# TensorE drains as release points: what message products, pairs and gathers wait for in a graph-network kernel

## The chip, the core and the metric

The kernel runs on one core of a Trainium2 chip. The core has five engines with a queue of their own each: TensorE (PE) for matrix products, VectorE (DVE), ScalarE (ACT), GpSimd (POOL) and SyncE (SP). They tell each other of finished work by semaphores. Sixteen DMA engines move data. The metric is the device time of one execution in microseconds (us), lower is better.

## The reference: what is computed

One message-passing block on a graph of 1,250 nodes with 512 features each (3 x 128 vector parts and 128 scalars) and 40,000 edges sorted by their target node, then a residual with layer norm:

```python
def _painn_block(x, edge_index, edge_attr1, edge_attr2, W1, b1, W2, b2, W3, b3, U, V, ...):
    x_j = x[src]
    v_j = x_j[:, :384].reshape(E, 128, 3)
    s_j = silu(x_j[:, 384:] @ W1 + b1) @ W3 + b3
    rbf = jnp.sqrt(2.0 / R_CUT) * jnp.sin(n * jnp.pi * r / R_CUT) / r
    cutoff = 0.5 * (jnp.cos(jnp.pi * r / R_CUT) + 1.0) * (r < R_CUT)
    edge_basis = rbf * cutoff @ W2 + b2            # 20 -> 384 for each edge
    s1, s2, s3 = split of (s_j * edge_basis)
    v_msg = v_j * s1[:, :, None] + s3[:, :, None] * edge_attr1[:, None, :]
    x = x + segment_sum([v_msg, s2], dst)          # first pass over the edges
    x_j = x[src]                                   # second pass: per node, then per edge
    v, v_V, norm, h = ...                          # U, V, a small network on (norm, s)
    msg = [v * s1, dot(v, v_V) + s3]               # depends on the source node alone
    return x + segment_sum(msg, dst)
x = layernorm(x + block(x, ...))
```

The second pass sends a row that depends on the source node alone. So the kernel doesn't gather for it: during the first pass it counts the links between nodes into a matrix, and multiplies the nodes' rows by these counts later.

## The kernel before, in words

**Tiling.** The 40,000 edges are cut into 80 batches (NT), of four tiles of 128 edges as a rule. Four batches make a group, and two groups a block of 128 target nodes. For each tile POOL issues one indirect DMA (`gather`, L756) that fetches 128 source rows of 640 numbers (2,560 bytes) from a table in device memory into one of five rooms in SBUF, which are parts of the tiles `more` (three) and `nodes` (two). POOL gathers three batches ahead.

**One step of the main loop** (step t, within `windowed`; its loop is at L1701) does this:

- DVE, `messages(t)`: the product of the gathered scalars with the edge factors (L916) and that of the vector parts (L918). Both read the factors from PSUM, where there is one set of four banks, `eb`. Then DVE compares numbers to make `pair` (L939, for the links; there are two buffers), `hot` (L847) and `spread` (L859, both for the additions).
- PE, `add_messages(t-1)`: 4 + 12 products (L955, L961) that sum the messages by target into `agg`. Their left sides are one-hot matrices of 32 columns.
- PE, `count_links(t-1)`: four products (L984) that count links into `adj`; L976 carries the part that two groups share. In the steps that the set `behind` holds, this stands after the factors and gathers, in all others before them.
- PE, `edge_factors(t+1)`: four products, one for each tile (L906; each runs in two parts in the profile's count, so "x8"), that write the next batch's factors to `eb`. They can't start before L918 of step t has read the banks.
- POOL, `gather(t+3)`: four gathers. The first of them waits for the last product of `edge_factors(t+1)`, and for the addition that last read the room.

Around these stand lists of further work (`first`, `early`, `late`, `mid`, `dve`, `amid`) that close a group (ACT copies the sums, L997 to L1024), turn the next edges' basis (L823, L828) and run the node network (L1051 to L1360). ACT also makes the one-hot matrices `one` from L871 and L881 for the links.

**What sets the order.** Each engine runs its own instructions in the order in which the program writes them. A tile library adds the semaphore waits from what is read and written; a wait that an engine has already passed at a later count isn't added again. A product that somebody waits for raises a semaphore of PE's (PE_49) when it completes. For the last three batches there are two smaller sets of banks (`halves`).

## Time and profile before

| | |
|---|---|
| Median of 3 runs | 569.23 us (568.55 to 569.3) |
| The profiled execution's own time | 567.24 us |
| Its span in the profile | 565.4 us |
| Granted clock of TensorE, mean | 0.907 |
| PE busy | 444.6 us (79%) |
| DVE busy | 432.1 us (76%) |
| ACT busy | 377.0 us (67%) |
| POOL busy | 350.1 us (62%) |
| Gather queue's packets, share of the 16 DMA engines | 62.6% |

The profile is of one execution. "Span" is the time from its first to its last instruction; what lies around it, 567.24 less 565.4 us, is 1.84 us. An engine's busy time leaves out waits. Ends of matrix products are modelled, not seen, so what a product's waiters did tells more of its end than its own row. A row of the timeline gives the start, the duration, the engine, the line, what is written and read, and in brackets how long the engine had been idle and what ended that. "issue" there means that the profile shows nothing that was waited for, "remote" that no releaser on this core was found. Granted clock 1.00 is PE's full speed; in parts of the span less is granted.

### The profile page before, as it was taken

To read this page: it belongs to the slowest core of one execution; us is meant where nothing else is said; L and a number is where in the kernel's file an instruction comes from. 1 tells how busy PE (TensorE), PEld (TensorE's weight loads), DVE (VectorE), ACT (ScalarE), POOL (GpSimd) and SP (SyncE) were. 2 spreads that over 40 slices of the span, in tenths; PEclk is the share of its full clock that TensorE was granted. 3 is DMA by queue.
4 is the path that set the end of the run, shared out by engine and by line. 5 is a ranking of instruction groups with operands and counts; after the bars stand their busy time and mean duration, and the time that the engine had idled before them with its cause. 6 is when DMAs were issued, how large, how long until landed. Compare 5 with 4: busy or idle time off the path is not lost.

```text
span 565.4 us, 11226 instructions
## 1 busy us (share of the span) xinstructions
PE 444.6 (79%) x4257; PEld 249.3 (44%) x4257; DVE 432.1 (76%) x660; ACT 377.0 (67%) x955; POOL 350.1 (62%) x377
## 2 busy tenths in 40 slices
PE   8557667677878787767887797879789698989993
PEld 6323233353344344435433443545445354445682
DVE  5576687778877877886778778787878887797675
ACT  3493565567777566775757687577768766788663
POOL 7775666666666666665556665666666666574530
PEclk9856998979897979988788897999989999999997
DMA  8786777777777776776777787678778777877413
GB/s 247 269 243 188 227 228 221 226 214 227 234 222 203 239 223 214 228 230 192 209 217 217 205 258 231 193 234 250 220 237 229 236 224 223 265 217 237 157 56 133
DMA packets 37938, 123.29 MB, mean 218 GB/s; under 512 B 7296, under 2 KB 9870, under 8 KB 37874
## 3 DMA queue, kind: packets, MB, share of 16 engines
q0 software_dynamic: 25824, 104.47, 62.6%
q1 hardware_dynamic: 10850, 17.35, 9.3%
q8 instruction: 35, 0.57, 0.4%
q10 hardware_dynamic: 1200, 0.66, 0.4%
q14 instruction: 29, 0.24, 0.2%
HBM read 112.94 MB, written 9.51 MB: 217 GB/s over the span
## 4 chain that ended last, share of the span: by engine, by line
PE 55%; DVE 20%; ACT 13%; issue 6%; another core or an unknown queue 3%; DMA 2%; POOL 0%; SPq 0%; DVEq 0%; POOLq 0%
PE eb L906 11%; PE agg L955 8%; PE agg L961 6%; DVE more L918 5%; PE adj L984 5%; PE begun L1359 5%; ACT one L881 5%; DVE nodes L918 4%; DVE more L916 3%; PE work L1146 3%; DVE nodes L916 3%; PE work L1051 2%; PE work L823 2%; ACT one L871 2%
## 5 line engine op out<-in xcount | busy, mean ns | idle before, releaser
L756 POOL DMA_INDIRECT more<-table,src_i x189 | 188.8, 999 | 106.2 <-issue 43.0
L756 POOL DMA_INDIRECT nodes<-table,src_i x124 | 123.5, 996 | 68.4 <-issue 28.6
L881 ACT ACTIVATE one<-one,weight,src_f 128x128 f16<-128x128 f16 x313 | 128.6, 483 | 0.2
L916 DVE TENSOR_TENSOR more<-more,eb 128x1024 f32<-128x1024 f32 (+2 forms) x48 | 57.2, 1193 | 63.8 <-PE eb L906 29.9
L871 ACT ACTIVATE one<-number,low 128x128 f16<-128x128 f16 x313 | 99.8, 393 | 6.9 <-remote 4.6
L906 PE MATMUL eb<-w_sb,basis_t 21*128 21x384 f32 x614 | 78.9, 577 | 29.4 <-DVE more L918 14.5
L918 DVE TENSOR_TENSOR more<-more,eb 128x1536 f32<-128x1536 f32 (+2 forms) x48 | 81.8, 1705 | 0.0
L916 DVE TENSOR_TENSOR nodes<-nodes,eb 128x1024 f32<-128x1024 f32 x30 | 36.6, 1222 | 39.4 <-PE eb L906 21.3
L955 PE MATMUL agg<-more,hot 128*32 128x512 f32 x378 | 61.7, 687 | 5.2 <-ACT sums L1006 5.2
L961 PEld LDWEIGHTS agg<-more,spread 128*32 128x32 f32 x1134 | 39.6, 119 | 37.8 <-issue 36.6
L984 PE MATMUL adj<-pair,one 128*128 128x160 f16 x313 | 38.0, 243 | 22.6 <-DVE basis L814 18.7
L918 DVE TENSOR_TENSOR nodes<-nodes,eb 128x1536 f32<-128x1536 f32 x30 | 52.4, 1747 | 0.0
L961 PE MATMUL agg<-more,spread 128*32 128x128 f32 x1134 | 48.6, 291 | 2.7 <-issue 2.7
L906 PEld LDWEIGHTS eb<-w_sb,basis_t 21*128 21x128 f32 x614 | 26.5, 198 | 51.9 <-issue 22.8
L859 DVE TENSOR_TENSOR spread<-hot,carried 128x384 f32<-128x384 f32 (+1 forms) x81 | 44.4, 549 | 2.7
L955 PE MATMUL agg<-nodes,hot 128*32 128x512 f32 x248 | 40.6, 658 | 3.9 <-ACT sums L1006 3.8
L984 PEld LDWEIGHTS <-one 128*128 128x128 f16 x313 | 23.4, 103 | 38.3 <-issue 36.4
L939 DVE TENSOR_TENSOR pair<-number,column 128x640 f16<-128x640 f16 (+1 forms) x81 | 38.7, 479 | 0.0
L961 PEld LDWEIGHTS agg<-nodes,spread 128*32 128x32 f32 x744 | 25.5, 118 | 23.1 <-issue 22.7
L961 PE MATMUL agg<-nodes,spread 128*32 128x128 f32 x744 | 31.8, 289 | 1.0 <-issue 0.9
L828 ACT COPY basis_t<-work 128x512 f32<-128x512 f32 x20 | 11.7, 587 | 29.6 <-PE adj L984 12.3
L1359 PE MATMUL begun<-upper,cast 128*128 128x512 f32 x57 | 28.1, 493 | 0.2 <-ACT cast L1350 0.2
(289 smaller groups left out, 711.2 us busy)
## 6 DMA issues: line engine op xcount, KB each, us to landing
table<-more SPq DMA_DIRECT2D x10, 320.0 KB
more<-table,src_i POOLq DMA_INDIRECT x189
spilled<-begun SPq DMA_DIRECT2D x10, 256.0 KB
more<-spilled SPq DMA_DIRECT2D x2, 1280.0 KB
node_x<-in_x_dram SPq DMA_DIRECT2D x35, 64.0 KB
nodes<-table,src_i POOLq DMA_INDIRECT x124
out_dram<-more SPq DMA_DIRECT2D x7, 256.0 KB
nodes<-in_x_dram POOLq DMA_DIRECT2D x2, 768.0 KB
```

Of the source, the lines that this page charges most:

```text
L756: got = nc.gpsimd.indirect_dma_start(out=rows_t[:n, j, :], out_offset=None, in_=sh.table1, in_offset=bass.IndirectOffsetOnAxis(ap=sh.src_i ...
L859: nc.vector.tensor_mul(spread[t][:m, js], hots[t][:m, js, None, :].to_broadcast(shape), sh.attr[:m, g, e : e + n, :, None].to_broadcast(sh ...
L871: nc.scalar.activation(onehots[t][:, j, :], number[:, :P], AF.Abs, bias=low[:, e : e + 1])
L881: nc.scalar.activation(one, one, AF.Relu, scale=less[:, e : e + 1], bias=worth[:, e : e + 1])
L906: made = nc.tensor.matmul(made_in[t][:, j, :V], turned[g][rows, i, :], sh.w2_sb[rows, :], start=True, stop=True,)
L916: nc.vector.tensor_mul(msg[:m, js, V:], msg[:m, js, V:], factors_of(t, js)[:m, :, C:V])
L918: nc.vector.tensor_mul(msg[:m, js, :V].rearrange("p t (k c) -> p t k c", k=3), msg[:m, js, :V].rearrange("p t (k c) -> p t k c", k=3), fac ...
L939: nc.vector.tensor_tensor(pair[:m, js, :].rearrange("p t (l h) -> p t l h", h=2), number[:m, : PARTS * WIN].rearrange("p (l h) -> p l h", ...
L955: nc.tensor.matmul(agg[j * WIN : (j + 1) * WIN, :], hots[t][:, j, :], msg[:, j, :width], start=(i == 0), stop=False, skip_group_check=True,)
L961: nc.tensor.matmul(agg[j * WIN : (j + 1) * WIN, c * C : (c + 1) * C], spread[t][:, j, c, :], msg[:, j, width:], start=False, stop=(i == la ...
L984: nc.tensor.matmul(to[:, :, at : at + WIN], one[:m, j, :], pair[:m, j, :].rearrange("e (p n) -> e p n", n=WIN), start=(i == 0 and j == js[ ...
L1359: nc.tensor.matmul(acc, casts[a, b], rows[:, a, :], start=(start and a == first and k == 0), stop=(stop and a == end - 1 and k == 1),)
```

## The change

PE gets a drain (`nc.tensor.drain()`), an instruction of its own that waits for the engine's work, behind each batch's factors (80 drains), and one behind the links' products in 33 steps: those before a step of the set `behind`, and the last ones. What waited for products waits for drains now:

- The message products (L916 and L918 before) are told not to depend on the factors' products, and wait for the drain.
- `pair` is told not to depend on the link products of two batches before, which read its buffer, and waits for their drain, or for that of its own batch's factors where there is none.
- All four gathers of a batch wait for the drain; before, the first alone waited for the last product. They are told not to depend on the additions that last read the room.

The order of the instructions stays the same on every engine; what they wait for differs. On POOL, the gathers of one batch stand so in the program of before (PE_49 is the semaphore that products raise, DMASW those of earlier gathers):

```order
L756 DMA more<-table_169,src_i 128x640 [waits DMASW2_49,DVE_49,PE_49]
L756 DMA more<-table_169,src_i 128x640 [waits DMASW3_49]
L756 DMA more<-table_169,src_i 128x640 [waits DMASW4_49]
L756 DMA more<-table_169,src_i 128x640 [waits DMASW5_49]
L756 DMA more<-table_169,src_i 128x640 [waits DMASW6_49,DVE_49,PE_49]
```

and so, from the eleventh batch on, in the changed one:

```order
L758 DMA more<-table_169,src_i 128x640 [waits PE_sequencer_49,DMASW2_49,DVE_49,PE_49]
L758 DMA more<-table_169,src_i 128x640 [waits DMASW3_49,PE_49]
L758 DMA more<-table_169,src_i 128x640 [waits DMASW4_49,PE_49]
L758 DMA more<-table_169,src_i 128x640 [waits DMASW5_49,PE_49]
L758 DMA more<-table_169,src_i 128x640 [waits PE_sequencer_49,DMASW6_49,DVE_49,PE_49]
```

PE_sequencer_49 is the semaphore that drains raise. The wait on PE_49 that each gather has now is for the last addition of a room's reader ten batches earlier. On DVE, a step's work begins so in the program of before:

```order
L916 TENSOR_TENSOR more<-more,eb_403 128x4x256 [waits DMASW6_49,DMASW1_49,DMASW7_49,DMASW0_49,PE_49]
L918 TENSOR_TENSOR more<-more,eb_403 128x4x384
L814 TENSOR_TENSOR basis<-turn,adj 128x16x20 [waits PE_49,Activation_49]
L939 TENSOR_TENSOR pair<-number,column 128x640
L847 TENSOR_TENSOR hot<-lane,carried 128x128
L859 TENSOR_TENSOR spread<-hot,carried 128x384 [waits DVE_49]
```

and so in the changed one:

```order
L931 TENSOR_TENSOR more<-more,eb_403 128x4x256 [waits DMASW6_49,DMASW1_49,DMASW7_49,DMASW0_49,PE_sequencer_49]
L935 TENSOR_TENSOR more<-more,eb_403 128x4x384
L819 TENSOR_TENSOR basis<-turn,adj 128x16x20 [waits PE_49,Activation_49]
L956 TENSOR_TENSOR pair<-number,column 128x640 [waits PE_sequencer_49]
L852 TENSOR_TENSOR hot<-lane,carried 128x128
L864 TENSOR_TENSOR spread<-hot,carried 128x384 [waits DVE_49]
```

In other steps `pair` waits for a link product itself (PE_49), in 40 of them where 21 did before. Of the additions (L987 in the changed kernel) 280 raise the semaphore, where 26 did. The factors' drain is L917 there, the links' L1017.

```diff
--- before.py
+++ after.py
@@ -742,6 +742,7 @@
 
         rows_of, msgs, onehots, turned, hots, spread = {}, {}, {}, {}, {}, {}
         aggs, adjs, pairs = {}, {}, {}
+        makers, tells, adders, counters = {}, {}, {}, {}
 
         sync = mybir.DependencyInfo(mybir.DependencyClass.Sync, mybir.DependencyReason.DATA)
 
@@ -751,6 +752,7 @@
 
             g, i = batches[t]
             rows_t = next(rooms)
+            past = t - len(sh.rooms)
             for j in tiles(g, i):
                 n = lanes(g, i, j)
                 got = nc.gpsimd.indirect_dma_start(
@@ -761,11 +763,14 @@
                         ap=sh.src_i[:n, g, i * CPG + j : i * CPG + j + 1], axis=0
                     ),
                 )
-                if behind is not None and j == 0:
-                    tc.add_manual_dep(
-                        got.ins, behind.ins.name, sync,
-                        reason="so that rows come while PE is ahead of DVE",
-                    )
+                if behind is None:
+                    continue
+                tc.add_manual_dep(
+                    got.ins, behind.ins.name, sync,
+                    reason="so that rows come while PE is ahead of DVE",
+                )
+                for made in adders.get(past, ()):
+                    tc.declare_no_dep(got.ins, made.ins, reason="a later drain is waited for")
             clear_rest(t, rows_t, nc.gpsimd)
             rows_of[t] = rows_t
 
@@ -901,25 +906,37 @@
 
         def edge_factors(t):
             g, i = batches[t]
+            makers[t] = []
             for j in tiles(g, i):
                 rows = slice(j * FEAT, j * FEAT + N_RBF + 1)
                 made = nc.tensor.matmul(
                     made_in[t][:, j, :V], turned[g][rows, i, :], sh.w2_sb[rows, :],
                     start=True, stop=True,
                 )
-            return made
+                makers[t].append(made)
+            tells[t] = nc.tensor.drain()
+            return tells[t]
+
+        def behind_drain(t, reader):
+            for made in makers[t]:
+                tc.declare_no_dep(reader.ins, made.ins, reason="a drain behind them is waited for")
+            tc.add_manual_dep(
+                reader.ins, tells[t].ins.name, sync, reason="TensorE drains behind a batch's factors"
+            )
 
         def messages(t):
             g, i = batches[t]
             msg = rows_of.pop(t)
             for js, n, m in runs(g, i):
-                nc.vector.tensor_mul(msg[:m, js, V:], msg[:m, js, V:], factors_of(t, js)[:m, :, C:V])
+                behind_drain(t, nc.vector.tensor_mul(
+                    msg[:m, js, V:], msg[:m, js, V:], factors_of(t, js)[:m, :, C:V]
+                ))
             for js, n, m in runs(g, i):
-                nc.vector.tensor_mul(
+                behind_drain(t, nc.vector.tensor_mul(
                     msg[:m, js, :V].rearrange("p t (k c) -> p t k c", k=3),
                     msg[:m, js, :V].rearrange("p t (k c) -> p t k c", k=3),
                     factors_of(t, js)[:m, :, None, :C].to_broadcast([m, n, 3, C]),
-                )
+                ))
             run(amid, t)
             make_pair(t)
             if t == 0:
@@ -936,7 +953,7 @@
             for js, n, m in runs(g, i):
                 e = g * EPG + i * CPG + js.start
                 shape = [m, n, PARTS * WIN // 2, 2]
-                nc.vector.tensor_tensor(
+                compared = nc.vector.tensor_tensor(
                     pair[:m, js, :].rearrange("p t (l h) -> p t l h", h=2),
                     number[:m, : PARTS * WIN].rearrange("p (l h) -> p l h", h=2)[
                         :, None
@@ -944,6 +961,14 @@
                     column[:m, e : e + n, None, :].to_broadcast(shape),
                     op=ALU.is_equal,
                 )
+                if t - 2 in counters:
+                    made, drained = counters[t - 2]
+                    for mm in made:
+                        tc.declare_no_dep(compared.ins, mm.ins, reason="a later drain is waited for")
+                    tc.add_manual_dep(
+                        compared.ins, (drained or tells[t]).ins.name, sync,
+                        reason="TensorE drains behind a batch's links",
+                    )
             pairs[t] = pair
 
         def add_messages(t):
@@ -951,19 +976,20 @@
             if i == 0:
                 aggs[g] = ps_sum.tile([P, width], F32, name="agg")
             agg, msg, js = aggs[g], msgs.pop(t), tiles(g, i)
+            adders[t] = []
             for j in js:
-                nc.tensor.matmul(
+                adders[t].append(nc.tensor.matmul(
                     agg[j * WIN : (j + 1) * WIN, :], hots[t][:, j, :],
                     msg[:, j, :width], start=(i == 0), stop=False, skip_group_check=True,
-                )
+                ))
             for c in range(3):
                 for j in js:
-                    nc.tensor.matmul(
+                    adders[t].append(nc.tensor.matmul(
                         agg[j * WIN : (j + 1) * WIN, c * C : (c + 1) * C],
                         spread[t][:, j, c, :], msg[:, j, width:],
                         start=False, stop=(i == last_tile(g, j) and c == 2),
                         skip_group_check=True,
-                    )
+                    ))
 
         def count_links(t):
 
@@ -977,16 +1003,18 @@
                     to[:, :, : REACH - GSPAN], ident, passed.pop(g),
                     start=True, stop=False, skip_group_check=True,
                 )
+            made = []
             for j in js:
                 m = lanes(g, i, j)
                 at = j * SHARE
 
-                nc.tensor.matmul(
+                made.append(nc.tensor.matmul(
                     to[:, :, at : at + WIN], one[:m, j, :],
                     pair[:m, j, :].rearrange("e (p n) -> e p n", n=WIN),
                     start=(i == 0 and j == js[0] and g == 0), stop=(i == last_tile(g, j)),
                     skip_group_check=True,
-                )
+                ))
+            counters[t] = made, nc.tensor.drain() if t + 1 in behind or t + 2 >= NT - 3 else None
 
 
         def close_group(g):
```

## The prediction

> **What bounds the kernel now.** I read the head of the profile's page first, with its chain of waits (the columns of the engine rows: busy time, share of the span, instructions).
>
> ```profile
> span 565.4 us, 11226 instructions
> PE 444.6 (79%) x4257; PEld 249.3 (44%) x4257; DVE 432.1 (76%) x660; ACT 377.0 (67%) x955; POOL 350.1 (62%) x377
> PEclk9856998979897979988788897999989999999997
> PE 55%; DVE 20%; ACT 13%; issue 6%; another core or an unknown queue 3%; DMA 2%; POOL 0%; SPq 0%; DVEq 0%; POOLq 0%
> ```
>
> No engine is full; the chain goes round between PE and DVE. So a step is waited for, rather than an engine being short. The table of busy times by stretch tells how long a batch takes. Its columns: the stretch and its length, then busy us (and instructions) of PE, PE's weight loads, DVE, ACT and POOL, the granted clock, the DMA engines' share and GB/s.
>
> ```profile
> 35.00:515.00 480.00, 380.83 (x3922) 204.78 (x3921) 374.74 (x528) 328.67 (x848) 308.03 (x312) 0.91 0.76 224
> 187.10:193.12 6.02, 4.38 (x37) 2.04 (x37) 4.58 (x6) 2.55 (x7) 3.84 (x4) 1.00 0.81 237
> 193.12:199.22 6.10, 4.52 (x56) 1.99 (x54) 5.69 (x9) 5.87 (x16) 4.16 (x4) 1.00 0.76 235
> 205.37:212.28 6.91, 6.42 (x52) 3.59 (x52) 4.71 (x6) 4.71 (x13) 3.82 (x4) 0.55 0.74 209
> 224.44:230.52 6.08, 5.28 (x59) 3.21 (x60) 4.84 (x7) 5.89 (x14) 3.83 (x4) 1.00 0.74 220
> ```
>
> The first row is the main loop: 312 gathers in 480 us, four to a batch, so 78 batches of 6.15 us, with PE busy 380.83/78 = 4.88 us in each. The other rows are single batches. At the full clock a batch takes 6.0 to 6.1 us whether PE has 4.4 or 5.3 us of work in it; only at the lower clock (0.55) does PE fill it, 6.42 of 6.91. A clock of 0.91 on average, with 0.55 where it is low, means 0.09/0.45 = a fifth of the loop, some 14 batches of 6.9 us; the other 64, at 6.0 us, make up the 480.
>
> What holds those 64 at 6.0 us is in the timeline (start, duration, engine, line, operation; in brackets the idle time before it and what ended that).
>
> ```profile
> 187.36 1.22 DVE L916 TENSOR_TENSOR nodes<-nodes,eb 128x1024 f32<-128x1024 f32 x1 [1.18 <-remote]
> 187.59 0.96 POOL L756 DMA_INDIRECT more<-table,src_i  x1 [1.11 <-remote]
> 188.50 1.75 DVE L918 TENSOR_TENSOR nodes<-nodes,eb 128x1536 f32<-128x1536 f32 x1
> 188.86 0.96 POOL L756 DMA_INDIRECT more<-table,src_i  x1 [0.30 <-issue]
> 190.12 0.96 POOL L756 DMA_INDIRECT more<-table,src_i  x1 [0.30 <-issue]
> 190.30 0.93 PE L906 MATMUL eb<-w_sb,basis_t 21*128 21x384 f32 x8 [1.33 <-issue]
> 191.15 1.12 PE L1051 MATMUL work<-sums,sel 128*128 128x512 f32 x2
> 191.39 0.96 POOL L756 DMA_INDIRECT more<-table,src_i  x1 [0.30 <-issue]
> 192.47 1.12 PE L1051 MATMUL work<-sums,sel 128*128 128x512 f32 x2 [0.19 <-issue]
> 193.38 1.22 DVE L916 TENSOR_TENSOR more<-more,eb 128x1024 f32<-128x1024 f32 x1 [1.40 <-PE work L1051]
> 193.61 0.96 POOL L756 DMA_INDIRECT more<-table,src_i  x1 [1.27 <-PE work L1051]
> ...
> 196.58 0.48 DVE L939 TENSOR_TENSOR pair<-number,column 128x640 f16<-128x640 f16 x1
> 196.83 0.93 PE L906 MATMUL eb<-w_sb,basis_t 21*128 21x384 f32 x8
> 199.48 1.22 DVE L916 TENSOR_TENSOR more<-more,eb 128x1024 f32<-128x1024 f32 x1 [0.38 <-PE adj L984]
> ...
> 202.42 0.93 PE L906 MATMUL eb<-w_sb,basis_t 21*128 21x384 f32 x8 [0.67 <-DVE more L918]
> 205.63 1.22 DVE L916 TENSOR_TENSOR more<-more,eb 128x1024 f32<-128x1024 f32 x1 [0.99 <-remote]
> ...
> 211.55 0.93 PE L906 MATMUL eb<-w_sb,basis_t 21*128 21x384 f32 x8
> 212.40 1.06 PE L955 MATMUL agg<-more,hot 128*32 128x512 f32 x8
> 212.54 1.22 DVE L916 TENSOR_TENSOR nodes<-nodes,eb 128x1024 f32<-128x1024 f32 x1 [2.17 <-PE eb L906]
> ```
>
> The factors of a batch (L906) end by the page at 191.23, 197.76 and 203.35; the message product that reads them (L916) starts at 193.38, 199.48 and 205.63: 2.15, 1.72 and 2.28 us later, though DVE was idle for 1.40, 0.38 and 0.99 us of it, and POOL's first gather starts 0.23 us behind DVE. The wait is credited to products that came after L906, or to "remote", since L906 had long been done. In the slow-clock batch the gap is 0.06 us (212.48 to 212.54). So **the signal of a product, not the product, is late** in the full-clock batches. That results lie ready sooner is likely, though not shown. The view of line L916 by releaser says how much of DVE's waiting this is:
>
> ```profile
> L916 DVEq EVENT_SEMAPHORE  x157: 21/50/3945, 32.3 to 522.9; - x157
>   PE eb L906: 51.2, 30
>   remote: 16.4, 14
>   PE adj L984: 10.9, 13
>   PE begun L1359: 9.0, 7
>   PE work L1051: 7.0, 5
> ```
>
> The last four rows, 43.3 us in 39 batches, are idle time that ended with something other than the factors.
>
> **The change part by part.** The sum is made against the profiled execution, 567.24 us (span 565.4); the median of the runs, 569.23, is 2.0 above it, which I add at the end. No instruction changes place; waits and drains are all that is new. L917, L956, L758, L987 and L1017 are lines of the changed kernel, all others those of the one before.
>
> *Factors' drain (L917, 80 of them) and the message products behind it.* Gain per batch at the full clock: 6.0 less what limits it next. The ring through the one set of factor banks is L916 and L918, 187.36 to 190.25, then L906 to 191.23: 3.87 us, and the drain's own time, not the limit. POOL is: four gathers of 0.96 + 0.30 make 5.04, and 0.23 to restart behind a signal gives 5.3. DVE has 4.58 to 5.69 us of work, ACT up to 5.89. So a plain batch can lose at most 0.7 us, and one like the two rows with ACT at 5.9 only 0.1 to 0.2; ACT's mean, 328.67/78 = 4.2 us, says that these are few, and I take a quarter. Upper bound: 48 x 0.7 + 16 x 0.2 = 37 us; lower: 0, if the drain tells nobody sooner. I take 0.5 and 0.15, as PE's 5.28 and a drain make some 5.5 in the fuller batches: 24 + 2 = **26 us less**. The 43.3 us of late releases above have room for that.
>
> *The same drains on PE.* No row shows a drain between products. Bounds: nothing where PE waits anyway (1.33 us ahead of L906 at 190.30), and 2.15 us if it lasts as long as the signal does. Nearest is the gap of 0.19 us at 192.47, where products do not follow without a seam; with the first weight load no longer under the product before it (0.08 us of overlap between L906's end at 212.48 and L955's start at 212.40) about 0.3 us. At the full clock this lies in PE's idle 0.8 to 1.6 us of a batch. In the 14 slow-clock batches PE is nearly full: 14 x 0.3 = **4 us more**. Queued behind a drain stand the additions of a batch (L955) or, as here, a closing group's products (L1051), and ACT's copies of the sums wait for those.
>
> *Links' drain (L1017, 33).* Of the same price, in the steps where links stand behind factors, so a second seam for PE: 33 x 0.3 = 10 us if nothing covers it, hidden where PE has 0.8 us to spare, and a fifth of the steps are slow-clock ones: **2 us more**.
>
> *Pairs (L956).* 9 wait for a drain. But 40 now wait on the last link product of two batches before (21 did), since the message product ahead of them no longer waits on a later product for them. That link product precedes the factors on PE, and the pair stands 2.97 us of L916 and L918 behind the drain, more than the 2.28 us of the latest signal above: nothing. Without that cover it would be the difference, and L847 and L859 of the next batch are queued behind.
>
> *Gathers (L758) and rooms.* All four of a batch now wait for the drain, not the first alone; the later three find it done. Besides, each waits for a count of the additions (L987) of the reader of its room, long past. The built program has 269 more event waits on POOL's queue over both of its branches. Two rows of the gathers' line price one:
>
> ```profile
> L756 POOLq EVENT_SEMAPHORE  x88: 17/43/5350, 25.8 to 511.4; - x88
>   issue: 71.6, 235
> ```
>
> At 0.043 us, four to a batch: 0.17 us, or 78 x 0.17 = 13 us if they stand in line; nothing if the queue runs them under the gather before, in its 0.96 us. The 0.30 us ("issue" is 71.6/235) has room for one, so I take **1 us**.
>
> *Increments.* Additions that signal go from 26 to 280, 254 more, because gathers count them. No row shows an increment's cost; bounds: nothing, and one product's slot each (24 narrow additions in 0.84 us, 0.035 each, from the row below), 9 us of PE. PE has more idle time than that, so nothing.
>
> ```profile
> 213.29 0.84 PE L961 MATMUL agg<-more,spread 128*32 128x128 f32 x24
> ```
>
> The Trainium skill has a price, in "TensorE: Matmul & The Clock Gate", section "The cost: per-tile semaphore tail": increments serialize, about 26 ns each. By it the term would be 254 x 0.026 = 6.7 us of PE, inside my bounds, and the sum 7 us later at most.
>
> Sum: -26 + 4 + 2 + 1 = -19; 567.2 - 19 = 548, and 2 for the median: **550 us**.
>
> **The rivals.** *A drain lasts as long as the signal is late* (slower). What speaks for it: nothing shows that L906 is really done at 191.23, since ends of products are modelled, and if PE itself is late, draining can't be early. Against it: the release at 193.38 is credited to the second L1051, which by the page runs until 193.59; so signals of products that stand 2 us apart come together, as from work long done. Place: PE, behind L906. Price: 1.7 to 2.3 us by the three gaps, less PE's idle time of a batch, 0.8 to 1.6 (mean 6.0 - 4.88 = 1.1): 0.25 us a batch if the late ends overlap idle time that was there anyway, up to 1.2 if none does. It decides from a drain of about 1.1 us on. 64 x 0.25 = 16 us, up to 77; I'd expect the lower end, 569 + 16 = **585 us**.
>
> *A drain's signal is no earlier than the last product's* (same or slower). Then there is nothing to gain at L916, and the bubbles stay: 4 + 2 + 1 = 7 us at my prices, none where PE's idle time covers all of them: 569 to **576 us**. For it: if the delay lies on the way of a signal out of PE, a drain's goes the same way. Against it: the slow-clock row with 0.06 us, where the way was no longer.
>
> The Trainium skill speaks for this rival, in "PSUM — Partial Sum Buffer", section "Engine vs sequencer instructions": an increment attached to the matmul fires when it completes, and a drain is for a standalone barrier and waits until the engine is fully idle. By that rule a drain comes later than the product, never sooner, and this kernel would have been better off before. The rows of 1.72 to 2.28 us don't agree with the first half of it in the full-clock batches, that of 0.06 does; no run here shows the second half.
>
> *POOL's waits stand in line* (less gain): at 0.17 us a batch the floor of 5.3 becomes 5.47, and if a restart behind a sequencer's signal costs 0.23 us once more, 5.7. The gain falls to 64 x 0.3 = 19 less 7 for drains: **555 to 560 us**. Against it: the gathers follow each other at 1.27, 1.26 and 1.27 us with their DMA waits, with no trace of them.
>
> **How the numbers follow.** Forecast, with the gain at 0.5 us a batch: 0.55. POOL in line: 0.06. A drain no earlier: 0.17, of which 0.07 within 0.2% and 0.10 slower. A long drain: 0.22. So faster 0.61, same 0.07, slower 0.32; 0.2% is 1.1 us, about what a measurement of this kernel can tell from no change. The likeliest case's own range goes from the upper bound of the gain with drains free, 569 - 37 = 532, to a gain of 0.2 us a batch, 569 - 13 + 7 = 563. As the drain's price is open downwards too (a faster ring could let the 14 slow-clock batches shrink by their idle 0.5 us, 7 us), the low end is 525. Upwards it takes in the second rival and the centre of the first: 588. What is left out, the longer drains above all, is some 0.15.
>
> **What would show it.** Right: the message product starts within 0.4 us of its factors' end, or as soon as DVE is free, and "PE adj L984", "PE work L1051" and "remote" leave the list of its releasers; plain batches of 5.3 to 5.6 us in the table by stretch; POOL's idle time ahead of a first gather falls from 1.1 to 1.3 us to about 0.5; PE's idle time behind factors is near 0.3 us. Wrong: the gap stays near 2 us and POOL's idle time with it (second rival); PE stands 1 us or more behind each drain and the additions and sums come later (first rival); gathers further apart than 1.27 us (third). A lower granted clock with a busier PE would take gain back: each hundredth of the mean is worth 480 x 0.01 = 5 us where PE is the bound. My weakest step is that a drain's signal takes another way than a product's.

## The result and the profile after

The changed kernel takes **617.11 us** (median of 4 runs, 615.4 to 617.81) where the kernel before takes 569.14 (568.55 to 569.3): a ratio of **1.084, 95% interval 1.0817 to 1.0864**. It is 48 us slower. The forecast was 550 us, with a range from 525 to 588: the time lies above the range, and the sign is wrong too. Here and below, medians are of all runs, while a ratio and its interval leave out executions that ran slower as a whole, and a ratio can differ by up to 0.3% from the quotient of the medians.

The head of the page after, of an execution of 617.29 us:

```profile
span 615.5 us, 11650 instructions
PE 462.1 (75%) x4257; PEld 254.6 (41%) x4257; DVE 431.3 (70%) x660; ACT 377.0 (61%) x955; POOL 349.9 (57%) x377
PE 32%; issue 19%; ACT 15%; DVE 9%; PEldq 8%; PEld 7%; another core or an unknown queue 3%; DMA 2%; POOL 0%; DVEq 0%; POOLq 0%; ACTq 0%
```

DVE, ACT and POOL have the same busy time as before to within a microsecond: most of the 50 us more of span (615.5 for 565.4) are waits. PE's 17.5 us more go with a lower granted clock, 0.862 for 0.907. In the chain "issue" went from 6% to 19%, and PE's sequencer (PEldq), which runs the drains, is new with 8%.

Two batches on the timeline after (columns as in the prediction; here and below, rows of other work that stand between are left out):

```profile
211.01 1.22 DVE L931 TENSOR_TENSOR more<-more,eb 128x1024 f32<-128x1024 f32 x1 [2.27 <-PEq L917]
211.82 0.95 POOL L758 DMA_INDIRECT nodes<-table,src_i  x1 [3.14 <-PEq L1017]
212.15 1.75 DVE L935 TENSOR_TENSOR more<-more,eb 128x1536 f32<-128x1536 f32 x1
213.08 0.95 POOL L758 DMA_INDIRECT nodes<-table,src_i  x1 [0.30 <-issue]
214.34 1.19 POOL L758 DMA_INDIRECT nodes<-table,src_i  x1 [0.30 <-issue]
214.98 0.93 PE L912 MATMUL eb<-w_sb,basis_t 21*128 21x384 f32 x8
215.83 1.09 POOL L758 DMA_INDIRECT nodes<-table,src_i  x1 [0.30 <-issue]
217.69 1.22 DVE L931 TENSOR_TENSOR more<-more,eb 128x1024 f32<-128x1024 f32 x1 [1.60 <-PEq L917]
217.72 0.71 PE L1011 MATMUL adj<-pair,one 128*128 128x160 f16 x4 [1.81 <-issue]
218.50 0.95 POOL L758 DMA_INDIRECT nodes<-table,src_i  x1 [1.58 <-PEq L1017]
```

Three things stand in these rows. The factors (L912) end at 215.91 by the page, and the message product starts at 217.69, **1.78 us later**, as before (1.72 to 2.28): the drain tells DVE no sooner than the product did. PE starts its next product 0.03 us behind DVE, after 1.81 us without work by the modelled ends: it starts nothing before the drain is over. And the first gather starts **0.81 us** behind the message product (211.82 and 218.50), where it was 0.23 before. The brackets of these two gathers name the links' drain (L1017), which raises the same semaphore and ends just then; a version without links' drains, below, has the same late start (0.85 us).

The views of lines L931, L917 and L758 (durations in ns: shortest, median, longest; then what ended the idle time before them):

```profile
L931 DVEq EVENT_SEMAPHORE  x158: 21/50/2725, 31.1 to 571.0; - x158
  PEq L917: 146.7, 74
L917 PEldq DRAIN  x80: 925/3162/4598, 34.1 to 567.0; - x80
L758 POOLq EVENT_SEMAPHORE  x356: 17/17/7510, 24.6 to 557.4; - x178
```

DVE waited 146.7 us ahead of L931 for the drain, where before it had waited about 103 us ahead of L916, all rows of its list together. A drain lasts 3.2 us (median) from when PE's sequencer reaches it.

### The profile page after: what moved, and what is told of

Its sections match the earlier page's. It is cut to its first block, busy times and chain, and to the rows that moved or that the text cites. A ratio compares the mean times of both kernels' runs of the same rounds, so it can differ in the third digit from the quotient of the medians.

```text
span 615.5 us, 11650 instructions
## 1 busy us (share of the span) xinstructions
PE 462.1 (75%) x4257; PEld 254.6 (41%) x4257; DVE 431.3 (70%) x660; ACT 377.0 (61%) x955; POOL 349.9 (57%) x377
## 4 chain that ended last, share of the span: by engine, by line
PE 32%; issue 19%; ACT 15%; DVE 9%; PEldq 8%; PEld 7%; another core or an unknown queue 3%; DMA 2%; POOL 0%; DVEq 0%; POOLq 0%; ACTq 0%
PEldq L917 7%; PE agg L981 6%; ACT one L886 5%; PE eb L912 4%; PE agg L987 4%; PE begun L1387 3%; ACT one L876 3%; PEld agg L987 3%; DVE more L935 3%; PE adj L1011 2%; PE work L1147 2%; DVE nodes L935 2%; DMA more<-table,src_i 1%; DVE nodes L931 1%
## 5 line engine op out<-in xcount | busy, mean ns | idle before, releaser
L758 POOL DMA_INDIRECT more<-table,src_i x189 | 188.9, 1000 | 133.5 <-issue 50.6
L758 POOL DMA_INDIRECT nodes<-table,src_i x124 | 123.7, 998 | 88.0 <-issue 30.2
L931 DVE TENSOR_TENSOR more<-more,eb 128x1024 f32<-128x1024 f32 (+2 forms) x48 | 57.2, 1193 | 96.7 <-PEq L917 92.9
L912 PE MATMUL eb<-w_sb,basis_t 21*128 21x384 f32 x614 | 78.1, 562 | 8.7 <-DVE more L935 5.6
L931 DVE TENSOR_TENSOR nodes<-nodes,eb 128x1024 f32<-128x1024 f32 x30 | 36.6, 1221 | 53.8 <-PEq L917 53.8
L981 PE MATMUL agg<-more,hot 128*32 128x512 f32 x378 | 66.5, 773 | 9.0 <-issue 7.8
L987 PEld LDWEIGHTS agg<-more,spread 128*32 128x32 f32 x1134 | 41.6, 132 | 41.7 <-issue 40.5
L1011 PE MATMUL adj<-pair,one 128*128 128x160 f16 x313 | 40.1, 257 | 21.5 <-issue 10.6
L987 PE MATMUL agg<-more,spread 128*32 128x128 f32 x1134 | 50.1, 317 | 0.0
L1011 PEld LDWEIGHTS <-one 128*128 128x128 f16 x313 | 25.0, 108 | 39.9 <-issue 38.4
L912 PEld LDWEIGHTS eb<-w_sb,basis_t 21*128 21x128 f32 x614 | 26.7, 194 | 29.7 <-issue 15.4
L1387 PE MATMUL begun<-upper,cast 128*128 128x512 f32 x57 | 30.2, 531 | 7.5 <-issue 6.8
L987 PEld LDWEIGHTS agg<-nodes,spread 128*32 128x32 f32 x744 | 24.8, 120 | 23.9 <-issue 23.8
L1079 PE MATMUL work<-sums,sel 128*128 128x512 f32 x36 | 24.7, 811 | 10.7 <-issue 9.5
```

The lines of the kernel that those rows point to most:

```text
L758: got = nc.gpsimd.indirect_dma_start(out=rows_t[:n, j, :], out_offset=None, in_=sh.table1, in_offset=bass.IndirectOffsetOnAxis(ap=sh.src_i ...
L912: made = nc.tensor.matmul(made_in[t][:, j, :V], turned[g][rows, i, :], sh.w2_sb[rows, :], start=True, stop=True,)
L931: behind_drain(t, nc.vector.tensor_mul(msg[:m, js, V:], msg[:m, js, V:], factors_of(t, js)[:m, :, C:V]))
L981: adders[t].append(nc.tensor.matmul(agg[j * WIN : (j + 1) * WIN, :], hots[t][:, j, :], msg[:, j, :width], start=(i == 0), stop=False, skip ...
L987: adders[t].append(nc.tensor.matmul(agg[j * WIN : (j + 1) * WIN, c * C : (c + 1) * C], spread[t][:, j, c, :], msg[:, j, width:], start=Fal ...
L1011: made.append(nc.tensor.matmul(to[:, :, at : at + WIN], one[:m, j, :], pair[:m, j, :].rearrange("e (p n) -> e p n", n=WIN), start=(i == 0 ...
```

## The experiments

All times are compared with runs of the kernel before on the same chip; where no interval is given, it is a single run. The edits are shown shortened, and some of the comments in them are this text's. The table is made from the traces: the medians over 70 batches of the main loop of how long after the message product the first gather starts, and of how long the batch is, from one message product to the next. The last column is the second less the first: from the first gather to the next message product. Line numbers shift by a few between versions.

| version | ratio to before (interval) | first gather after message product, us | batch, us | difference, us |
|---|---|---|---|---|
| before | 1 | 0.24 | 6.10 | 5.87 |
| the change | 1.084 (1.0817 to 1.0864) | 0.81 | 6.77 | 5.97 |
| drains alone | 1.0213 (1.0158 to 1.0269) | 0.24 | 6.13 | 5.90 |
| change, gathers on the product | 1.0162 (1.0095 to 1.0228) | 0.19 | 6.13 | 5.94 |
| before, gathers on the drain | 1.0779 (1.0733 to 1.0824) | 0.85 | 6.78 | 5.93 |
| change, no waits on old additions | 1.0732 (1.0646 to 1.0819) | 0.71 | 6.61 | 5.90 |
| before, POOL starts later | 1.0553 (1.0483 to 1.0623) | 1.30 | 7.15 | 5.86 |
| before, half the rows | no interval | 0.24 | 6.11 | 5.87 |
| before, fewer additions | no interval | 0.24 | 6.11 | 5.87 |

### Which part of the change costs what

**Drains alone:**

```diff
+            nc.tensor.drain()                 # behind edge_factors' products
             return made
...
+            if t + 1 in behind or t + 2 >= NT - 3:
+                nc.tensor.drain()             # behind count_links' products
```

> The kernel before with all 113 drains of the change in their places, and nobody waiting for them: every wait, and each product's increment, is as before. Theory A (the drains keep PE from starting the next additions while the last ones still run, so they cost by themselves): most of the 48 us, 600 to 617 us. Theory B (the gathers restart 0.8 us instead of 0.23 us behind their release, 0.58 us x 78 batches = 45 us, and the drains lie in time that PE had anyway): 569 to 578 us.

581.15 us for 567.79 (576.84 to 582.98): 13 us, a quarter of the loss and a little over theory B's upper end. The drains cost by themselves, but they are not the main thing.

**The change with its gathers as before:**

```diff
-                if behind is None:
-                    continue
-                tc.add_manual_dep(got.ins, behind.ins.name, sync, ...)
-                for made in adders.get(past, ()):
-                    tc.declare_no_dep(got.ins, made.ins, ...)
+                if behind is not None and j == 0:
+                    tc.add_manual_dep(got.ins, behind.ins.name, sync, ...)   # behind: the last product
```

> The changed kernel with its gathers as before: the first of a batch waits for the last factor product, the others for nothing new, and the additions' increments fall away with that; message products and pairs still wait for drains, all 113 drains stay. Theory A: 600 to 617 us, like the change. Theory B: 569 to 578 us, and the first gather starts 0.23 us behind the product's signal.

578.73 us for 567.79: 11 us. This kernel has all the drains, and message products and pairs behind them. It isn't distinguishable from the drains alone, so waiting on a drain instead of a product brings the message products nothing that these runs can tell. What the gathers' edit costs is the rest, 48 - 11 = **37 us**.

**The kernel before with factor drains and the changed gathers:**

```diff
+            return nc.tensor.drain()          # edge_factors
...
                 # gather: all four behind the drain, no dependence on adders[t - 5], as in the change
```

> The kernel before with factor drains (80) and the changed gathers alone: all four of a batch wait for the drain, with the additions' increments that follow from it; no links' drains, message products and pairs wait for products as before. Theory A: the price of 80 drains, about 0.7 of the 48 us, 595 to 605 us. Theory B: 610 to 617 us, like the change, with the first gather 0.8 us behind the drain.

610.79 us for 567.79, ratio 1.0779: 43 us from 80 drains and the gathers alone, as theory B had it.

### Why the first gather starts later

On POOL, some waits are instructions of their own ("POOLq EVENT_SEMAPHORE") that stand ahead of the gather, and the last is part of the gather itself. In the program before, the gather itself waits for PE, and its one event ahead (an old DMA's and DVE's semaphores) was through long before. In the changed one the drain's wait is an event; a second event stands behind it, and then the gather with a wait on an old addition. The next run takes the old additions out:

```diff
-                for made in adders.get(past, ()):
+                for made in [m for u in range(past, -1, -len(sh.rooms)) for m in adders.get(u, ())]:
                     tc.declare_no_dep(got.ins, made.ins, reason="a later drain is waited for")
```

> The changed kernel without the gathers' waits on old additions: these are declared as no dependence for all earlier readers of a room, not only the last, so their increments go too (282 signalling products for 533). A first gather has one event wait (its DMA semaphore and the drain) and then waits itself for DVE only, in the changed kernel two event waits and a wait of its own. If the instructions that stand behind the release on POOL's queue are what the change lost (0.57 us a batch), half or more of the 38 us between the change and the run with gathers on the product comes back: 580 to 600 us. If the drain as a release is what costs, 610 to 617 us.

610.03 us for 566.92 on its chip, ratio 1.0732 (1.0646 to 1.0819), and the gather 0.71 us behind the message product. That is outside the 580 to 600 us, and within the range for a drain that costs as a release. The waits on old additions and 251 increments (282 signalling products for 533) make only 0.10 us of the delay. The other 0.47 us stay, though one event and one gather are all that is left. The event waits in the view of the gathers' line show the difference, first in the kernel before, then in this run:

```profile
L756 POOLq EVENT_SEMAPHORE  x88: 17/43/5350, 25.8 to 511.4; - x88
```

```profile
L758 POOLq EVENT_SEMAPHORE  x89: 17/4716/7027, 25.7 to 552.4; - x89
```

and this run's timeline:

```profile
210.56 1.22 DVE L931 TENSOR_TENSOR more<-more,eb 128x1024 f32<-128x1024 f32 x1 [0.64 <-PEq L917]
211.27 0.96 POOL L758 DMA_INDIRECT nodes<-table,src_i  x1 [1.82 <-issue]
```

There is one event a batch in both. Its median was 43 ns, so it wasn't the place where POOL waited; here it is 4.7 us, so it is. Nor does the drain's word reach POOL late: in this trace the event that carries it ends within 0.01 us of the start of the message product, which waits for the same drain (median of 70 batches), and the gather starts 0.70 us behind the event, in all but a few of them to the hundredth. The time is lost between the event and the gather. **A gather that carries the last wait itself starts 0.24 us behind the release; one that stands behind an event which carries it starts 0.71 us behind.** That, and not how many waits there are, is most of the 37 us: the 0.57 us by which the change starts its gathers later, of which this is 0.47, make 36 us in the prediction's 64 batches at the full clock. Why a gather needs 0.70 us behind an event isn't shown.

To see whether a late gather alone costs that, without drains, the next run only puts small clears ahead of the first gather:

```diff
+            if behind is not None:
+                late = pool.tile([16, 128], F32, name="late", bufs=1)
+                for k in range(3):
+                    held = nc.gpsimd.memset(late, 0.0)     # the first one waits for the factor product
```

> The kernel before with three small clears (16 x 128) on POOL ahead of the first gather of each batch; the first of them waits for the factor product in the gather's place. No drain, no other wait. Theory G: each batch gets longer by what the clears put ahead of the first gather, one for one: for 0.5 to 0.6 us, 77 x that is 39 to 46 us, 606 to 615 us. Theory P: POOL has over a microsecond of idle time in each batch, so nothing, 567 to 572 us.

602.85 us for 572.91: 30 us. The clears put 1.06 us ahead of the gather, not 0.5 to 0.6:

```profile
220.99 1.22 DVE L924 TENSOR_TENSOR nodes<-nodes,eb 128x1024 f32<-128x1024 f32 x1 [2.53 <-PE eb L914]
221.07 0.70 POOL L757 MEMSET late<- 16x128 f32 x3 [1.12 <-PE eb L914]
222.29 0.96 POOL L764 DMA_INDIRECT more<-table,src_i  x1 [0.52 <-issue]
226.07 0.96 POOL L764 DMA_INDIRECT more<-table,src_i  x1 [0.30 <-issue]
226.55 1.66 PE L914 MATMUL eb<-w_sb,basis_t 21*128 21x384 f32 x8
228.28 1.22 DVE L924 TENSOR_TENSOR nodes<-nodes,eb 128x1024 f32<-128x1024 f32 x1 [2.82 <-PE eb L914]
```

POOL is idle for over a microsecond of each batch (1.12 us here), and yet starting it later costs. The median batch grows by 1.05 us, one for one with the gather; the mean grows by 0.45 only, since in 22 of the 70 batches the next factors' signal came out in the middle of the burst, after 5.1 us on average (2 of 70 in the change, none before). So the rule holds for the median batch but not for the whole kernel, where it forecasts some 80 us.

### What makes a batch 5.87 us from its first gather

The last column of the table hardly moves: from the first gather to the next message product it is 5.86 to 5.97 us, whatever the drains, waits or delays. So the kernel runs in a ring: POOL's first gather waits for a release by PE, and PE's next release comes 5.87 us behind that gather. A wait for the fetched rows is not what ends it: in the kernel before, the list of what ended DVE's idle time ahead of L916 names no DMA (one wait of 3.3 us, of 103 in all, was for one by the view of the gathers' line), and in two batches of the prediction's timeline (187.36 and 205.63) the rows had landed 4.5 to 4.9 us earlier. Five runs looked for what that stretch consists of. "Theory P" is that PE is really full and its modelled ends too early, "theory G" that the gathers set it.

```diff
-            for c in range(3):                # fewer additions: 8 of 12 narrow ones left out
+            for c in range(2, 3):
```

> The kernel before without 8 of the 12 narrow additions of a batch (two of three vector parts are left out of the sums), so PE has 0.55 us less in each batch by the model, and more if the additions really take longer than modelled. Theory P (PE is really full, its ends are modelled too early, and that is why its signals come late): the batch falls by 0.5 us or more, 569 - 40 = 530 us or less. Theory G (PE's signals are held until some 2.1 us after the start of the last gather; the batch is 0.24 + 3 x 1.26 + 2.1 = 6.1 us, whatever PE does): within 6 us of 569.

570.09 us for 572.91; the median batch is 6.11 us, as before, and PE is busy for 366 of the loop's 480 us where it was for 381. Theory P falls. (The mean granted clock was lower in this run, 0.836; why isn't shown.)

```diff
-                    out=rows_t[:n, j, :],      # short rows: 512 bytes for 2,560
-                    in_=sh.table1,
+                    out=rows_t[:n, j, :128],
+                    in_=sh.table1.rearrange("r (a c) -> (r a) c", c=128),
...
-                n = lanes(g, i, j)             # half the rows (another run)
+                n = min(lanes(g, i, j), 64)
```

> The kernel before, with gathers of 128 instead of 640 numbers for each row (512 bytes for 2,560, from other addresses; so messages are wrong and the DMA traffic of the main loop falls to a fifth), all else alike. If rows that land hold the additions up (they took 3.5 to 5.6 us by their signals in the changed kernel, 1.84 us in the one batch with no landings, 1.72 us by the model), the signals of products come with their modelled ends, and a batch falls from 6.0 us to POOL's 5.3: 515 to 530 us. If traffic has nothing to do with it, signals stay about 2 us late and the time within 5 us of 569.

> The kernel before with four gathers of 64 instead of 128 rows for each batch (the other half of the edges isn't fetched and its rows hold zeros): half the descriptors. If POOL's issue of a gather is what holds PE's signals, and its 0.96 us doesn't depend on the rows, the batch stays at 6.1 us: 565 to 575 us. If the hold is the descriptors' way through the DMA engines, it shrinks by half, some 1 us a batch: 490 to 510 us.

574.68 and 581.04 us, for 567.79 and 566.88: both a little longer, with median batches of 6.10 and 6.11 us. (They also clear the rooms once at the start. With half the rows the mean batch is longer too, 6.4 us for 6.2, which isn't explained.) A fifth of the bytes doesn't shorten the batch, nor do half the rows. One batch with half the rows:

```profile
231.15 0.92 POOL L758 DMA_INDIRECT more<-table,src_i  x1 [2.11 <-PE eb L908]
232.37 0.91 POOL L758 DMA_INDIRECT more<-table,src_i  x1 [0.30 <-issue]
233.59 0.91 POOL L758 DMA_INDIRECT more<-table,src_i  x1 [0.30 <-issue]
234.58 0.93 PE L908 MATMUL eb<-w_sb,basis_t 21*128 21x384 f32 x8
234.80 0.98 POOL L758 DMA_INDIRECT more<-table,src_i  x1 [0.30 <-issue]
237.04 1.22 DVE L918 TENSOR_TENSOR more<-more,eb 128x1024 f32<-128x1024 f32 x1 [1.28 <-PE work L1185]
```

The factors end at 235.51, the message product starts at 237.04: 1.53 us, 5.89 us behind the first gather.

```diff
-            for j in tiles(g, i):
+            for j in tiles(g, i)[:1]:          # one gather; [:2] in the run with two
```

> The kernel before with one gather instead of four for each batch (three of four tiles aren't fetched, their rooms hold zeros). Theory G: 0.24 + 2.1 = 2.3 us no longer bounds a batch; the signals of factor products come near their modelled ends, and what is left is DVE and PE at some 4.9 us and ACT where a group closes: 480 to 515 us. Theory P: the batch stays near 6 us and signals stay 2 us late: 560 to 570 us.

> The kernel before with two gathers instead of four for each batch (the other two tiles aren't fetched, their rooms hold zeros). If a signal is held until 2.1 us after the start of whatever gather was last, signals still come 2.1 us after the second one, and the batch isn't bound by it (0.24 + 1.26 + 2.1 = 3.6 us): 480 to 500 us. If the hold grows with the number of gathers in a row, it is well under 2.1 us here, with the same time.

**476.58 us with one gather a batch, 478.09 with two**, for 572.91 and 566.88. The granted clock was higher as well, 0.952 and 0.948; but batches at the full clock took 6.0 to 6.1 us before, so the clock alone doesn't make a batch shorter. In the run with two:

```profile
205.86 0.95 POOL L758 DMA_INDIRECT more<-table,src_i  x1 [0.30 <-issue]
209.37 0.93 PE L908 MATMUL eb<-w_sb,basis_t 21*128 21x384 f32 x8
210.59 1.20 POOL L758 DMA_INDIRECT more<-table,src_i  x1 [3.79 <-DVE spread L861]
210.88 1.22 DVE L918 TENSOR_TENSOR more<-more,eb 128x1024 f32<-128x1024 f32 x1
```

The factors end at 210.30, and the gather that waits for them starts at 210.59, 0.29 us later (the bracket names `spread`, which ended 0.06 us behind them). The batch is 4.91 us (median), near what PE has to do in one on average before, 4.88 us, and DVE, 374.74/78 = 4.80. That two gathers cost about as little as one says that they lie under that work; four don't. Of the two theories G holds: the number of gathers, not their size and not PE's work, makes the 6.1 us.

The trace of the kernel before shows the rule that theory G guessed. In 10 of the 70 batches the factors end over 2.2 us behind the start of the last gather, and the message product starts 0.07 to 0.08 us behind them. In the other 60 it starts 1.86 to 2.17 us behind the start of the last gather, whenever the factors ended. The prediction's slow-clock batch is one of the ten; its last gather is this:

```profile
209.64 0.96 POOL L756 DMA_INDIRECT nodes<-table,src_i  x1 [0.30 <-issue]
```

Its factors end 2.84 us later, at 212.48, and are reported at once (0.06 us). In the runs with one and two gathers the factors end as far from a gather, and their reports are as prompt at the full clock. So the prompt report doesn't take a low clock.

### Can the ring be opened?

Four edits release gathers elsewhere; no drains are in them.

```diff
-                if behind is not None and j == 0:
+                if behind is not None and j == 0 and t < 5:     # free gathers
...
-        ahead = 3
+        ahead = 2                                               # (and, in another run, two batches ahead)
```

> The kernel before, with the wait of the gathers on the factor product taken out from the sixth batch on; the first gather of a batch still waits for its room. Theory G, if only the quiet after a burst lets signals out: POOL has no pause between bursts, signals come later still, and the time is 570 us or more. If signals need only the time since a given gather: the burst starts earlier by up to 1.3 us a batch, POOL's pace of 5.05 us is the floor, 500 to 545 us. Theory P: about as before.

573.56 us for 572.91, ratio 1.0029 (0.9993 to 1.0064): the same. Both theories allow that.

> The kernel before with gathers two batches ahead instead of three, and from the sixth batch on without the wait on the factor product: the first gather of a batch then waits only for its room, whose additions ran a batch earlier, so POOL has no pause between bursts. If a gather takes 1.47 us of something (5.87 us from the first gather of a batch to the release, over 4) and PE's signals come once it is through, POOL can't run faster than 5.87 us a batch: 545 to 555 us if signals get out without a pause. If they need a pause, message products wait longer and the time is 570 us or more.

572.56 us for 566.92, ratio 1.0103 (1.0058 to 1.0148): a little slower. In both, POOL runs ahead until its room stops it, and that wait is on PE as well. A row of the list of what ended POOL's idle time ahead of the gathers shows it, first of the run with free gathers, then of two ahead:

```profile
  PE agg L961: 27.9, 16
```

```profile
  PE agg L961: 37.2, 19
```

L961 are the additions that free a room; they are no releaser of gathers in the kernel before. These two runs don't fit the rule of 5.87 us: their median batches are 6.13 and 6.06 us, but the message product starts only 0.52 and 0.55 us behind its factors (1.55 before). The wait has moved: to the rooms, and in 10 and 8 batches to rows that hadn't landed (11.3 and 14.7 us). The library also adds event waits on POOL's queue for the rooms, 302 and 299 where there were 88. So they show that this edit gains nothing, and not what the limit is.

```diff
+        fetch(t, rows_t, js[:2], behind)             # two gathers at their old place
...
+                fetch_rest(t + 2, scaled)            # the other two a step later, behind L918 or L916
```

> The kernel before with the burst cut in two: the first two gathers of a batch wait for the factors as before, the other two are issued one step later and wait for the second message product (L918) of that step. All work is done, no drain. If the hold comes from four in a row, signals come soon after two, and the batch falls to POOL's 5.3 us or to the order of waits, some 5.6: 525 to 545 us. If any gather holds the signals for 2.1 us, the second pair starts 2.95 us behind the message product's start, ends its hold at 2.95 + 1.26 + 2.1 = 6.3 us, and the time is 570 to 590 us.

> The same with the second pair behind the first message product (L916), which ends 1.2 us after the release: on POOL the two pairs then follow each other like a burst of four that starts with the other batch's pair. Held by any gather: first pair from 0.24 us, second from 2.8 us, the last start at 4.0 us, plus 2.1: 6.1 us a batch, 565 to 575 us. Held by four in a row only, or by the number of rows of a batch: no other forecast than the same.

571.42 us for 566.88 behind L918 (1.0054, 1.0014 to 1.0093) and 566.89 behind L916 (1.0020, 0.9974 to 1.0067), with batches of 6.11 us in both (6.3 was forecast behind L918). Cutting the burst in two opens nothing. No version here beats the kernel before.

## Why the prediction was wrong, by its steps

- **"My weakest step is that a drain's signal takes another way than a product's."** It failed there first. The message product starts 1.78 us behind the factors in the rows above, and the run with gathers on the product shows no gain from 80 drains as releases. The 26 us that the sum rests on were never there: what holds a product's signal back holds the drain too. The reason that the prediction gave against this rival, the prompt report of the slow-clock batch, was misread: by the rule above that report is prompt because the last gather had started 2.84 us before the factors ended. The second rival had the rest right, at 0.17, and with 0 to 7 us for the drains; they cost 11 to 13.
- **"POOL is: four gathers of 0.96 + 0.30 make 5.04, and 0.23 to restart behind a signal gives 5.3."** The rows for the gathers are right, but POOL's issue isn't what a batch waits for. It is 5.87 us from the first gather to the next release, so the limit of this ring is 6.1 us and the batches were already on it. The prediction's own rows had it: 6.0 to 6.1 us whatever PE held, with POOL idle 1.1 to 1.3 us. I put that down to late signals that could be sped up, and didn't ask what made the batches the same length to a tenth of a microsecond.
- **"I take 1 us"** for the gathers' waits. This is the term that was mis-sized, 37 us by the runs. The reasoning (an event of 0.043 us runs under the gather before) is right for waits that are long past: the median event after is 17 ns. It is wrong for the first event, which is now the one that waits for the release, with an event and the gather's own start behind it. I counted events, and should have asked which instruction carries the last wait.
- **The third rival (POOL's waits in line)** named the right place, at 0.06, but subtracted from a gain: I treated the rivals as excluding each other. The result is the second and third together: no gain at L916, and 0.57 us a batch on the ring. Its sign didn't show, though: the gathers of a batch still follow each other at 1.26 us (median), and the delay lies ahead of the first.
- **The first rival (a long drain)** was right that a drain lasts (3.2 us by its row, PE idle for 1.81 us in the rows above), and wrong in price: 13 us with nobody waiting, not 16 to 77, since PE's idle time can cover most of it. The drains' terms, 4 + 2 us, were half of it.
- **Increments and pairs** at nothing: the run that takes 251 increments and the old waits away gives back 0.16 us of the median batch (6.77 to 6.61), by the ratios some 6 us of the whole, old waits included. No run tried the pairs alone; they wait 2.4 us in all for links' drains.
- **The Trainium skill's rule** ("PSUM — Partial Sum Buffer", section "Engine vs sequencer instructions"), that a drain waits until the engine is fully idle. The trace after agrees: behind 77 of the 80 factors' drains, PE starts nothing before the drain is over, in the rows above 1.78 us behind the modelled end of the factors. What the prediction inferred from it for the second rival, that a drain comes no sooner than the product, served better than my reading of the late rows. Those rows don't contradict the page, as I wrote: the ends in them are modelled, so they can't tell whether a late report followed a late end.

## What to carry to other kernels

When an engine idles in every batch and every batch still has the same length, look for a ring: measure from one engine's first issue to the next release, and leave work out on each side until the length moves. Before changing what an instruction waits for, look which instruction carries the wait that comes last; a wait that moved from a gather into an event ahead of it cost 0.47 us each time here, though neither shows as busy time. A drain was a barrier for its engine here, and no quicker word from it.

## What the runs showed of the hardware

**Gathers hold back TensorE's reports of finished products.** In the kernel before, the gather that waits for the factors starts 1.89 us behind their modelled end (median; 0.3 where nothing is held, 2.5 at most but for one). With one or two gathers a batch it is 0.30 us (0.28 to 0.31) in all but two batches of each run. Neither the bytes of a row (512 for 2,560) nor the rows (64 for 128) nor 8 narrow additions fewer on PE changes the batch of 6.1 us.

Two gathers hold reports back too; the factors only come too late to be caught. Take the products that signal and end within 1.5 us behind a gather's start, and the first report that the trace has behind each one's modelled end. With one gather a batch this report is over 0.2 us late for 2 of 85 products, with two for 50 of 128, with four for 148 of 175. For products that end over 2 us behind the latest gather's start it is late in none of the three (18 products or more in each). The trace lacks some records, so the counts are rough. So one gather alone holds next to nothing, and what gathers hold is out some 2 us behind the last one's start.

In the trace of the changed kernel the reports of one batch's last four additions come one by one, long behind their modelled ends (times from the trace's semaphore records, on a clock that starts 0.24 us later than the page's):

```
 83.52 to 83.55  modelled ends of the last four additions (L987)
 83.77, 85.02, 86.28  the last three gathers of a burst start on POOL
 85.31, 86.01, 86.77, 87.47  the four additions' semaphore updates
 88.26  the factors' drain ends; the message product starts at 88.30
```

In one batch of that trace in which no gather started for over 5 us, the additions' last report came 1.84 us after their start, where the model has 1.72; in the others it was mostly 3 to 5.7.

The Trainium skill says in "SBUF — State Buffer", section "Who interferes with whom", that only the port pair that VectorE and GpSimd share causes contention; TensorE has no part in it. By that, gathers could not hold PE at SBUF's ports. Its reports are held here all the same, by the runs with one and two gathers against the kernel before; no run shows whether that goes against the page or takes another way, and what it is in a gather that does this stays open. So does whether PE computes on meanwhile and only its reports are held, or stops: the runs took gathers, bytes, rows and products away, but none separates the two.
